# Half of layer 0 over listed columns, one gather for adj and adj^T, norm roots on VectorE

## Chip, cores and metric

One core of a Trainium2 chip. The metric is the device time of one execution in microseconds (us), the median of several. The experiments ran in four calls, each on one chip (numbers 7, 12, 14 and 1, in this order), with seven runs of the kernel before beside them; ratios are to those of the same call. In the profile, PE is TensorE, PEld its weight loads, DVE VectorE, ACT ScalarE, POOL GpSimd, SP SyncE.

## The reference, cut to what matters

```python
# x: 4096 x 256, adj: 4096 x 4096, sparse, with a full diagonal
x = layernorm(x + adj @ (x * W0))                            # layer 0
R = (adj + I) / (adj + I).sum(-1)                            # layer 1, two steps n = 0, 1
for n in range(2):
    A  = top_p(softmax(q(Xa) @ k(Xa).T))                     # keeps a share of 0.9
    Xf = R @ Xf;  Xa = A @ Xa
    Z += Xf @ U1[n].T + Xa @ U2[n].T
x = layernorm(x + layernorm(x + Z) * g + b)
x = layernorm(x + masked_softmax(adj * (x @ Hv)) @ x)        # layer 2
x = layernorm(x + concat(x, adj @ x, edge) @ weight + bias)  # layer 3
#   edge[i] = sum_j adj[i, j] * adj[j, i]
```

adj is so sparse that, for a tile of 128 rows, all nonzero columns fit in 4 to 16 groups of 128 gathered rows. The kernel finds these columns itself ("lists") and multiplies only over them where it can.

## The kernel before

There are 32 row tiles. `CAPS` has the listed column groups of a tile: 16, 10, 8, 7, 7, 6, 7, 5, 6, 5 ... for the first, then 5, and 4 for the last eight. Layer 0 is dense (32 matmuls a tile) and notes on the way which columns are nonzero; attention step 0 then gathers the listed columns of adj^T (`pc`) and of adj (`pr`, needed for `edge`), saves `pc` to DRAM for later layers, and gathers the rows of the features (`xg`).

```python
def pack(I, ps):                       # attention step 0 only
    for m, (a, b) in enumerate(pieces(I)):            # pieces of up to 5 groups
        pc = pools["gat"].tile([P, PIECE, P], F32, name="pc", bufs=4)
        pr = pools["gat"].tile([P, PIECE, P], F32, name="pr", bufs=2)
        for k in range(a, b):
            gather(pc[:, k - a, :], adjT_r, idx_a, col(I, k))      # POOL
            gather(pr[:, k - a, :], adj_r, idx_a, col(I, k))       # POOL
        nc.sync.dma_start(packed[I][m], pc[:, :b - a, :])
        nc.vector.tensor_mul(pr[...], pr[...], pc[...])
        ...  # PE sums pr into edge
def listed_matmul(ps, src, width, I, parts, use=None):
    ...      # per group: gather xg (POOL, six buffers), then one PE matmul
def new_xf(I, psr, old):
    t = ...; nc.vector.tensor_add(t, psr[:, :D], old)
    nc.gpsimd.tensor_scalar_mul(xf, t, rinv[:, I:I + 1])           # POOL
def layernorm(o, y):
    ...      # statistics on VectorE
    nc.gpsimd.tensor_scalar_add(ve, mv[:, 1:2], EPS)               # POOL
    nc.gpsimd.tensor_tensor(rs, ve, neg_half, OP.pow)              # POOL
    nc.vector.tensor_scalar(o, y, mv[:, 0:1], rs, ...)
...
for I in range(NT):                    # step 0
    ...
    weighted_sum(psa, cur[0], X)                                    # PE, dense
    if I >= LAG[0]:
        out_f0(I - LAG[0], r_sum(0, I - LAG[0]))   # pack, listed_matmul, new_xf; PE transposes xf
```

The order of instructions on each engine is fixed when the kernel is built, by a scheduler that may bring an instruction forward past others of its engine.

## Time and profile before

Timed median 4069.91 us (4069.02 to 4073.49). The first profile was of a run of 4129.56 us; a later one spans 4069.7. Stages are read from the timeline: from the start of the ScalarE instruction that writes the first `xa` tile of a step, to the last, and to the last `y` of layer 3.

| stage | first profile | later profile |
|---|---|---|
| layer 0, lists, to the first xa of step 0 | 668.1 | 659.1 |
| step 0, first to last xa | 1183.4 | 1162.4 |
| passage to the first xa of step 1 | 167.2 | 165.3 |
| step 1 | 1510.8 | 1507.7 |
| layers 2 and 3 | 585.9 | 562.7 |

### The profile page before, as it was taken

Reading aid. Unit: us, or ns where it says so; the run is one execution under the profiler, and the core shown is the slowest. Engines: PE = TensorE matmul, PEld = TensorE weight load, DVE = VectorE, ACT = ScalarE, POOL = GpSimd, SP = SyncE. Lnnn points to the kernel's source line nnn. Section 1 sums busy time; section 2 is a strip of 40 time slices with the busy share of each in tenths; the row PEclk is TensorE's granted clock in tenths of the full one; section 3 lists DMA queues with packets and bytes.
Section 4 is the critical chain, followed back from the end, with each engine's and each line's share of the span. In section 5 each row is a group of like instructions: output and inputs, shape, how many; then the busy total and the mean of one; then the engine's idle time right before and its main releaser. Section 6 shows DMA issues by size and latency. Waiting matters only on the chain. (4 is left out here: it accounts for less than half of the span.)

```text
span 4127.7 us, 43235 instructions
## 1 busy us (share of the span) xinstructions
PE 3344.7 (81%) x12988; PEld 2304.1 (56%) x12988; DVE 2409.0 (58%) x7672; ACT 1250.7 (30%) x2837; POOL 1476.9 (36%) x1814
## 2 busy tenths in 40 slices
PE   7999978988889999996887788778888775555576
PEld 5777755656656666663555555445555544433354
DVE  4347446434345455533788888888888889133022
ACT  0000012322223233323444544444444442222011
POOL 1000032255455555524432222211111111577786
PEclk9999987978889999995788878877777877766688
DMA  6444431122222222212211111110000000355454
GB/s 176 141 141 141 141 104 29 45 64 59 63 74 65 66 65 70 66 36 75 74 51 38 39 34 36 35 31 30 29 29 27 27 21 13 114 171 164 129 162 122
DMA packets 291123, 309.34 MB, mean 75 GB/s; under 512 B 34624, under 2 KB 244048, under 8 KB 290880
## 3 DMA queue, kind: packets, MB, share of 16 engines
q1 hardware_dynamic: 234688, 177.31, 14.1%
q0 software_dynamic: 46976, 120.79, 10.4%
q10 hardware_dynamic: 9216, 8.39, 0.7%
q8 instruction: 105, 1.72, 0.2%
q14 instruction: 138, 1.13, 0.1%
HBM read 263.07 MB, written 43.29 MB: 74 GB/s over the span
## 5 line engine op out<-in xcount | busy, mean ns | idle before, releaser
L408 PE MATMUL lg<-kT,qi 64*128 64x512 f32 x1024 | 693.4, 809 | 36.2 <-ACT e L474 14.1
L191 ACT COPY eT<-pt 128x512 f32<-128x512 f32 x512 | 281.6, 588 | 1147.8 <-PE pt L189 1075.0
L213 POOL TENSOR_SCALAR ve<-mv 128x1 f32<-128x1 f32 x160 | 40.0, 250 | 1487.3 <-DVE mv L211 1473.0
L194 PE MATMUL acc<-xa,eT 128*128 128x256 f32 x2048 | 526.1, 414 | 26.3 <-ACT eT L191 26.1
L194 PE MATMUL acc<-x,eT 128*128 128x256 f32 x2048 | 508.9, 395 | 0.0
L178 PE MATMUL acc<-xw,panel 128*128 128x257 f32 x2048 | 483.1, 388 | 23.9 <-DVE xw L113 14.8
L194 PEld LDWEIGHTS acc<-xa,eT 128*128 128x128 f32 x2048 | 413.9, 208 | 129.4 <-ACT eT L191 56.6
L320 POOL DMA_INDIRECT xg<-xd,idx_x x360 | 366.3, 1018 | 281.5 <-PE acc L365 205.5
L189 PE MATMUL pt<-ident,e 128*128 128x128 f32 x2048 | 309.2, 298 | 162.4 <-DVE e L610 143.7
L194 PEld LDWEIGHTS acc<-x,eT 128*128 128x128 f32 x2048 | 378.4, 193 | 105.3 <-ACT eT L191 26.7
L365 PE MATMUL acc<-xg,pc 128*128 128x256 f32 x1080 | 362.3, 462 | 85.0 <-DVE y L668 55.1
L178 PEld LDWEIGHTS acc<-xw,panel 128*128 128x128 f32 x2048 | 379.7, 192 | 89.8 <-issue 26.4
L408 PEld LDWEIGHTS lg<-kT,qi 64*128 64x128 f32 x1024 | 206.1, 235 | 386.8 <-ACT junk L477 161.3
L474 ACT ACTIVATE e<-lg 128x512 f32<-128x512 f32 x512 | 305.6, 599 | 344.6 <-PE lg L408 250.8
L189 PEld LDWEIGHTS pt<-ident,e 128*128 128x128 f32 x2048 | 269.5, 155 | 230.4 <-DVE e L610 195.0
L547 DVE MAX8 cand<-e 128x8 f32<-128x128 f32 x1024 | 226.5, 280 | 287.0 <-ACT e L474 211.3
L320 POOL DMA_INDIRECT pr<-in_adj,idx_a x180 | 259.7, 1443 | 349.6 <-PE acc L339 307.1
L365 PEld LDWEIGHTS acc<-xg,pc 128*128 128x128 f32 x1080 | 230.0, 234 | 152.2 <-DVE y L668 66.7
L172 DVE TENSOR_REDUCE seen<-panel 128x4 bf16<-128x512 f32 x256 | 176.4, 690 | 236.1 <-DMA panel<-in_adjT 235.1
L365 PE MATMUL acc<-xg,pe 128*128 128x257 f32 x360 | 140.8, 566 | 139.8 <-issue 102.0
L204 ACT COPY xT<-ptx 128x256 f32<-128x256 f32 (+1 forms) x160 | 73.0, 456 | 546.8 <-DVE seen L172 283.1
L556 DVE MAX8 cand<-tmp 128x8 f32<-128x128 f32 x1024 | 203.9, 277 | 0.1
(221 smaller groups left out, 4567.9 us busy)
## 6 DMA issues: line engine op xcount, KB each, us to landing
panel<-in_adjT SPq DMA_DIRECT2D x256, 256.0 KB
z<-z SPq DMA_DIRECT2D x128, 128.0 KB
pc<-pk SPq DMA_DIRECT2D x51, 320.0 KB
pc<-pk SPq DMA_DIRECT2D x51, 256.0 KB
xin<-xd SPq DMA_DIRECT2D x96, 128.0 KB
xin<-in_x ACTq DMA_DIRECT2D x64, 128.0 KB
xg<-xd,idx_x POOLq DMA_INDIRECT x360
pk<-pc SPq DMA_DIRECT2D x17, 320.0 KB
```

What stands on the lines that cost most here:

```text
L172: nc.vector.tensor_reduce(seen[:, c * JC:(c + 1) * JC, I], a, AX.X, OP.max, apply_absolute_value=True)
L178: nc.tensor.matmul(ps[:, :width], a[:, k, :], r, start=(j == 0), stop=(j == NT - 1))
L189: nc.tensor.transpose(pt[:, k, :], e[:, j * P:(j + 1) * P], ident)
L191: nc.scalar.copy(eT, pt)
L194: nc.tensor.matmul(ps[:, :D], eT[:, k, :], rhs[j][:, :D], start=(j == 0), stop=(j == NT - 1))
L204: nc.scalar.copy(xT[:, :n, :], pt[:, :n, :])
L320: nc.gpsimd.indirect_dma_start(out=o, out_offset=None, in_=src, in_offset=bass.IndirectOffsetOnAxis(ap=idx[:, c], axis=0))
L365: nc.tensor.matmul(ps[:, :width], pc[:, k, :], xs[k][:, :width], start=(n == 0), stop=(n == CAPS[I] - 1))
L408: nc.tensor.matmul(ps, qi[r, :], kT[r, c * LC:(c + 1) * LC], start=True, stop=True)
L474: nc.scalar.activation(e[:, c * LC:(c + 1) * LC], ps, AF.Exp, accum_out=s8[:, c:c + 1])
L547: nc.vector.max(cand[:, g, :], e[:, g * SEG:(g + 1) * SEG])
L556: nc.vector.max(cand[:, c * (NS // 2) + g, :], w[:, g * SEG:(g + 1) * SEG])
```

## The change

Three parts. (1) Tiles 16 to 31 of layer 0 use lists too; their columns must then be known early, so 64 extra loads of 512 KB look for them during the first five dense tiles. (2) adj and adj^T are interleaved in DRAM (by the host, before the timed execution), so one gather of 1 KB rows brings both; tiles 16 to 31 are gathered in layer 0 and only reloaded in step 0. (3) the roots of the norms of layers 0, 2 and 3 become eight small VectorE operations, and one add of layer 3 moves to VectorE. In step 1 the norms stay on POOL.

```diff
 def pack(I, ps):
-            pc = pools["gat"].tile([P, PIECE, P], F32, name="pc", bufs=4)
+            pc = pools["gat"].tile([P, PIECE, 2, P], F32, name="pc2", bufs=4)
-                gather(pc[:, k - a, :], adjT_r, idx_a, col(I, k))
-                gather(pr[:, k - a, :], adj_r, idx_a, col(I, k))
+                gather(pc[:, k - a].rearrange("p s i -> p (s i)"), pair_r, idx_a, col(I, k))
-            nc.vector.tensor_mul(pr[:, :b - a, :], pr[:, :b - a, :], pc[:, :b - a, :])
+            nc.vector.tensor_mul(pr[:, :b - a, :], pc[:, :b - a, 0], pc[:, :b - a, 1])
@@ layernorm
+        if own:
+            nc.vector.tensor_scalar(ve, mv[:, 1:2], EPS, 0.5, op0=OP.add, op1=OP.mult)
+            nc.vector.tensor_scalar(rs.bitcast(I32), ve.bitcast(I32), -0.5, ..., op0=OP.mult, op1=OP.add)
+            for _ in range(3):
+                t = one("vt")
+                nc.vector.tensor_scalar(t, rs, rs, ve, op0=OP.mult, op1=OP.mult)
+                nc.vector.scalar_tensor_tensor(rs, t, 1.5, rs, op0=OP.subtract, op1=OP.mult)
@@ layer 0
+    def find_columns(J):
+        for b in range(LE, NT, HB):
+            t = pools["loads"].tile([P, HB, P], F32, name="half", bufs=3)
+            nc.scalar.dma_start(t, adjT_v[:, J, b:b + HB, 1])
+            nc.vector.tensor_reduce(seen[:, J, b:b + HB], t, ...)
-    for I in range(NT):
+    for I in range(LE):                    # LE = 16
         ...
+        for J in range(I * NEW, min((I + 1) * NEW, NT)):      # NEW = 7
+            find_columns(J)
+        if (I + 1) * NEW >= NT:
+            ...   # list_columns(1) once, then listed_0(late), one or two per dense tile
-        if I >= LE - 1: ...  three steps of list_columns(0) per tile
-    for _ in lists:
+    for _ in list_columns(0):
         pass
@@ r_sum
-        parts = pack(I, psr[:, D:D + 1]) if n == 0 else unpack(I)
+        parts = pack(I, psr[:, D:D + 1]) if n == 0 and I < LE else unpack(I)
@@ out_3
-        nc.gpsimd.tensor_add(t, t, x3)
+        nc.vector.tensor_add(t, t, x3)
```

## The prediction

> **What bounds the kernel now.** I read the page first, then stretches of the span (busy time of each engine, granted clock, DMA share), then the waits, then the timeline around one wait, and the chain of waits last. The page's second part tells that there are stages with different limits: 40 slices of 103 us.
>
> ```profile
> PE   7999978988889999996887788778888775555576
> DVE  4347446434345455533788888888888889133022
> POOL 1000032255455555524432222211111111577786
> PEclk9999987978889999995788878877777877766688
> DMA  6444431122222222212211111110000000355454
> ```
>
> Slices 1 to 6 are layer 0, dense over all 4096 columns (to 594.7 us in the trace). Slices 7 to 18 are attention step 0 (first output tile at 668.1, last at 1851.5), 19 and 20 the passage to step 1 (2018.7), then step 1 until 3529.5 with DVE at 8, then layers 2 and 3 with POOL at 7 to 8. The profile spans 4127.7 us, 1.4% over the timed 4069.91; I give trace microseconds and neglect that.
>
> By stretches (columns: start and end, length, then busy us of PE, PEld, DVE, ACT, POOL, then granted clock, DMA share, GB/s):
>
> ```profile
> 400.00:500.00 100.00, 95.71 (x462) 77.98 (x461) 41.59 (x91) 6.88 (x24) 4.86 (x12) 1.00 0.48 140
> 900.00:905.00 5.00, 0.04 (x1) 0.04 (x1) 0.28 (x2) 0.00 (x0) 3.97 (x5) 0.62 0.43 137
> 910.00:915.00 5.00, 5.00 (x7) 1.78 (x7) 2.25 (x11) 1.38 (x4) 0.00 (x0) 0.50 0.26 92
> 1300.00:1400.00 100.00, 98.98 (x459) 69.59 (x458) 55.40 (x184) 34.00 (x90) 45.24 (x43) 1.00 0.22 63
> 2100.00:2200.00 100.00, 76.37 (x268) 49.79 (x267) 82.22 (x270) 45.73 (x92) 23.34 (x35) 0.80 0.13 39
> 3900.00:4000.00 100.00, 67.51 (x258) 51.80 (x258) 20.66 (x56) 11.47 (x24) 81.20 (x100) 0.80 0.51 156
> ```
>
> Layer 0 is bound by PE, at full clock, with DMA near half. Step 0 at 1300 is bound by PE too, 33.9 us a tile. But at 900 PE stops, and afterwards it is "busy" at half clock. Who stopped it:
>
> ```profile
> 904.96 0.48 PE L202 MATMUL ptx<-ident,xf 128*128 128x128 f32 x1 [6.31 <-POOL xf L669]
> 925.98 0.94 POOL L320 DMA_INDIRECT pr<-in_adj,idx_a  x1 [16.16 <-PE acc L339]
> 929.11 4.48 DVE L587 SCALAR_TENSOR_TENSOR e<-e,f_u 128x4096 f32<-128x4096 f32 x1
> 929.82 4.59 POOL L320 DMA_INDIRECT pr<-in_adj,idx_a  x1 [0.30 <-issue]
> ```
>
> And in the table of waits (us in total, times, longest us):
>
> ```profile
> POOL pr L320 <- PE acc L339: 307.1, 27, 21.7
> ```
>
> PE waits for POOL's xf; POOL, in order, had been waiting for one of the two pr buffers, freed by PE. That wait came 27 times, 307.1 us in all. The result is visible in the distances of the output tiles: 33.9 us where five columns are listed, 46 to 54 us at tiles 5 to 11, 13 and 20, whose listed tile (about five behind) has 6 to 10.
>
> In layers 2 and 3 POOL issues gathers, and in layer 3 it also does small arithmetic between them:
>
> ```profile
> L828 POOL TENSOR_TENSOR y<-y,xin 128x256 f32<-128x256 f32 x32 | 23.4, 732 | 7.4 <-DVE y L827 6.8
> L213 POOL TENSOR_SCALAR ve<-mv 128x1 f32<-128x1 f32 x160 | 40.0, 250 | 1487.3 <-DVE mv L211 1473.0
> L215 POOL TENSOR_TENSOR rs<-ve,neg_half 128x1 f32<-128x1 f32 x160 | 93.7, 586 | 10.7
> ```
>
> The second number after the bar is the ns of one.
>
> **What the Trainium skill says.** "TensorE: Matmul & The Clock Gate", section Part 1 (the HAM clock gate): after an idle window of about 3.4 us the array runs at half clock until a busy one. Agrees in kind: 6.31 us of wait, then 0.50. The return took longer than one window here (0.50 still at 915 to 920, 1.00 at 935). "SBUF — State Buffer", section Who interferes with whom: a DVE instruction with two SBUF inputs contends with GpSimd's reads. The trace agrees: a gather takes 4.59 us beside the 4.48-us L587, else 0.95. "GPSIMD Engine Reference", section 4.1 Engine selection: elementwise work belongs on VectorE. Agrees: L828 takes 732 ns on POOL, an add of the same 128x256 on DVE (y L668) 409. "DMA: Bandwidth & Descriptors", section Issuing engines are not separate DMA queues: transfers issued by ACT and SP interleave on the same 16 engines. So the new loads on ACT's queue are no extra bandwidth; before has no such pair of heavy queues to check it.
>
> **The change part by part.**
>
> *Layer 0 (to first output tile, 668.1).* Removed: 16 dense tiles of 17.4 us (2.1 MB of panels a tile), 278 us of PE. Added: 16 listed tiles, 72 columns. One fp32 weighted matmul with 257 columns costs about 1.2 us (two records of 0.57), so 4.5 of them 5.4 us with the projection's part neglected, 88 us of PE in all. PE's work falls from about 560 to 370. But to know the columns of tiles 16 to 31, 64 loads of 512 KB come in tiles 0 to 4: 33.5 MB. With panels 5 x 2.1 (and prefetch, 11.8), x 4.9, the copy of xw 4.2 and weights 2, this is 56 MB. The rate at full share I estimate as 140/0.48 = 290 GB/s, so at least 193 us, and with imperfect overlap 225, where PE had needed 87. Then the chain of list_columns for the last 16 tiles: rounds of max and replace, 0.68 + 0.67 + gaps = 1.64 us, some 20 rounds and selections, 35 us, hardly beside anything: 260. Thereafter PE has 10 dense tiles (174) and 88 of listed, and waits at the start for POOL: a listed tile is 4 or 5 pair gathers and as many of xw, 1.25 us each back to back, and the first four hold PE about 20: end at about 541, against 594.7. But now list_columns for the first 16 tiles stands behind all of this, where before it was spread over the last tiles: 32 rounds x 1.64 = 52, and selections, 70 us; then 16 logit matmul groups and keep_few (27) and the weighted sum (28). First output tile at 541 + 125 = 666. Gain: 0, plus or minus 40. PE's saving is eaten by DMA and by the list.
>
> *Step 0.* Gathers per column on POOL fall from three to two for tiles 0 to 15, and to one for 16 to 31, which were gathered in layer 0. pr is no longer filled by a gather, so POOL doesn't wait for it. If PE then never stops, 4 tiles as before (125), 15 tiles x 33.9 + 17 columns over five x 0.69 = 520, the last 12 as before (383, of which 6 for the 40.2 of tile 29): 1028 against 1183, i.e. -155. xg keeps six buffers, which tiles of 7 to 10 columns will overrun, so some stops remain: -120 (35).
>
> *Passage to step 1*, 167 us: four tiles' pack, 16 columns, lose 32 gathers (pc and pr gone; loads from SP instead) x 1.25 = 40 us of POOL, which PE follows. -40 (20).
>
> *Step 1.* Bound by DVE (82%), its layer norms are left on POOL: 0 (10).
>
> *Layers 2 and 3.* Off POOL per tile: in layer 3 the add 0.73, ve 0.25, rs 0.59 and gaps, about 1.7; 32 x 1.7 = 54 at most. Gathers remain 180 x 1.25 = 225 us, so the floor is near 3812 + 225 + 10 and layer 3 ended at 4115: 54 fits in. In layer 2, 0.84 x 32 = 27 at most. DVE gains about 8 small operations, each some 0.15 to 0.2: 1.3 us a tile, at 20% busy it has room. PE has clock 0.80 and 67% busy in layer 3, so not all arrives: -70 (25) for both. The 43.72 us at 3807.50 in the chain of waits is POOL filling the first tiles' gathers of layer 3, and stays.
>
> Sum: 0 - 120 - 40 + 0 - 70 = -230. From 4070: 3840 us.
>
> **Rivals.** (1) Layer 0 gains as PE's work does, 150 us or so, because the loads overlap better than I think: ~3690. For it: DMA has half its share free. Against: 33.5 MB in 5 tiles, and all in order behind panels. (2) Layer 0 gets longer: the loads wait in ACT's in-order stream behind transposes that wait for PE, three buffers only, and PE's clock falls to half while it waits. End of the dense part at 580 to 620, total 3900 to 3930. (3) The waits in step 0 come from xg's buffers and the 4.5-us DVE instruction, not from pr: tiles 5 to 11 stay at 47 us, and the total is ~3950. Against: 307.1 us under pr in the waits, 217.9 under xg. (4) PE at half clock takes POOL's place in layers 2 and 3: +40 over my figure. I chose the middle since (1) and (2) pull in opposite directions.
>
> **Range and chances.** Four terms with 40, 35, 20, 25 give 62 if independent; 1.28 x 62 = 80, and some for what I overlooked: 3740 to 3930. Slower than 3988 (within 2%) needs two rivals together: faster 0.93, same 0.05, slower 0.02.
>
> **What would show it right or wrong.** Layer 0: DMA share above 0.85 and PE under half busy in the first 220 us, first output tile of step 0 near 666; under 600 rival 1, above 700 rival 2. Step 0: tiles 5 to 11 at 34 to 38 us, clock 1.00, no wait of POOL for pr; 47 would be rival 3. Passage near 127 us. Step 1 unchanged at 48.7 us a tile. Layer 3: POOL without L828, L213, L215, over 90% gathers, 6.3 us a tile instead of 8.0. Wrong altogether if POOL's gathers of 1 KB took longer than the 0.95 us of 512 B, which nothing here has measured (an xg row has 1 KB too and takes the same 0.95, so I don't expect it).

## The result

| | before | after |
|---|---|---|
| median us | 4071.7 (4069.02 to 4074.05, 4 runs) | 3967.85 (3963.28 to 3975.08, 4 runs) |
| ratio | | 0.9747, interval 0.9729 to 0.9765 |

A ratio is the mean time of a kernel's fast runs over that of the kernel before's fast runs in the same rounds, so not quite the ratio of the medians. Faster by 2.5%, but 104 us where 230 were forecast: 3967.85 lies outside 3740 to 3930.

Slices of the changed kernel's span, 99 us each (PE, clock and DMA alone):

```profile
PE   4767959998899999998877787878888776555677
PEclk9878977977789999998788878787777777866799
DMA  9956621122222111113211110011000000056565
```

The first two slices show DMA full and PE busy for 4 and 7 tenths; a new hole of PE comes in the sixth slice; slices 9 to 12, the early tiles of step 0, still have the clock at 7 to 8; in the last five PE has gained. The stages of the two kernels, both profiled on one chip (spans 4069.7 and 3972.0):

| stage | before | after | difference | predicted |
|---|---|---|---|---|
| layer 0 to first xa | 659.1 | 663.2 | +4 | 0 |
| step 0 | 1162.4 | 1150.3 | -12 | -120 |
| passage | 165.3 | 144.0 | -21 | -40 |
| step 1 | 1507.7 | 1502.7 | -5 | 0 |
| layers 2 and 3 | 562.7 | 500.9 | -62 | -70 |

One line fails badly: step 0. It misses 108 of the 134 us between these differences (96) and the forecast (230). In the waits (us in total, times, longest), before and then after, on that chip:

```profile
POOL pr L320 <- PE acc L339: 295.9, 27, 18.6
PE ptx L202 <- POOL xf L669: 112.4, 59, 14.3
```

```profile
POOL xg L336 <- PE acc L383: 729.4, 258, 24.4
PE ptx L207 <- POOL xf L711: 90.2, 58, 6.8
```

POOL's wait for `pr`, 296 us, on which the prediction was built, is gone altogether. POOL waits instead for xg's buffers (729.4; before it was 223.4). But PE's wait for xf, the one that costs, only went from 112.4 to 90.2. The timeline of the changed kernel shows how xf comes to be late (start, us, engine, line, instruction, and in brackets the idle time ahead of it with what ended it):

```profile
840.30 0.42 DVE L710 TENSOR_TENSOR y<-acc,xin 128x256 f32<-128x256 f32 x1 [3.22 <-PE acc L383]
...
840.83 0.95 POOL L336 DMA_INDIRECT xg<-xd,idx_x  x1 [0.30 <-issue]
842.08 0.96 POOL L336 DMA_INDIRECT xg<-xd,idx_x  x1 [0.30 <-issue]
843.35 0.95 POOL L336 DMA_INDIRECT xg<-xd,idx_x  x1 [0.31 <-issue]
844.60 0.95 POOL L336 DMA_INDIRECT xg<-xd,idx_x  x1 [0.30 <-issue]
845.58 0.94 POOL L711 TENSOR_SCALAR xf<-y,rinv 128x256 f32<-128x256 f32 x1
...
846.57 0.69 PE L207 MATMUL ptx<-ident,xf 128*128 128x128 f32 x2 [4.40 <-POOL xf L711]
```

y, from which POOL makes xf, is ready at 840.72. POOL first issues four more gathers, back to back 1.25 us apart, and comes to xf at 845.58; PE has then stood for 4.40 us. No wait is put down to POOL in these lines: it is simply busy with something else first. What it gathers there is told by the order of POOL's instructions as built, around this xf (buffer numbers show the tile: 5203 to 5211 belong to this one, 5467 to 5481 are the first six groups of the next):

```text
xg_5205<-xd, xg_5207<-xd, xg_5209<-xd, xg_5211<-xd
xg_5467<-xd, xg_5469<-xd, xg_5471<-xd, xg_5473<-xd, xg_5479<-xd, xg_5481<-xd
xf_5218<-y,rinv
pc2<-pair x3
```

So the next tile's gathers stand in front of this tile's xf. They can be issued only as PE's matmuls for this tile free the six buffers, hence at the very time at which xf is wanted. With 5 groups a tile this fits in; with 6 to 10 it mostly doesn't. Tile by tile, at tiles 5 to 11 and 13 xf starts 4.9 to 7.2 us after y is done, with four to six gathers in between; at all others it starts 0.2 to 1.6 us after it. In the kernel before (later profile) it is 3.7 to 8.5 us at tiles 5 to 11, 13 and 20, and at most 1.6 elsewhere: just the tiles that are slow. The clock then doubles the damage (stretch, length, busy of PE, PEld, DVE, ACT, POOL, granted clock, DMA share, GB/s):

```profile
840.00:850.00 10.00, 5.60 (x12) 2.17 (x11) 2.16 (x9) 2.44 (x7) 7.97 (x9) 0.66 0.41 125
850.00:860.00 10.00, 10.00 (x19) 4.53 (x19) 4.78 (x23) 3.10 (x10) 3.97 (x5) 0.50 0.44 126
```

After the 4.40 us PE is "busy" for 13 us and more at 0.50.

### The profile page after: what moved, and what is told of

It is laid out like the page before. It is cut to its first block, busy times and chain, and to the rows that moved or that the text cites. A ratio compares the mean times of both kernels' runs of the same rounds, so it can differ in the third digit from the quotient of the medians.

```text
span 3968.6 us, 41856 instructions
## 1 busy us (share of the span) xinstructions
PE 3189.8 (80%) x12108; PEld 2148.7 (54%) x12108; DVE 2520.8 (64%) x8408; ACT 1251.9 (32%) x2837; POOL 1198.3 (30%) x1482
## 5 line engine op out<-in xcount | busy, mean ns | idle before, releaser
L336 POOL DMA_INDIRECT xg<-xd,idx_x x360 | 386.4, 1073 | 654.0 <-PE acc L383 591.4
L383 PE MATMUL acc<-xg,pc 128*128 128x256 f32 (+1 forms) x1224 | 418.2, 463 | 144.1 <-DVE y L710 61.9
L383 PEld LDWEIGHTS acc<-xg,pc 128*128 128x128 f32 x1224 | 249.8, 229 | 245.9 <-DVE y L710 75.4
L183 PE MATMUL acc<-xw,panel 128*128 128x257 f32 x1024 | 284.1, 426 | 90.0 <-DVE xw L117 37.1
L230 POOL TENSOR_SCALAR ve<-mv 128x1 f32<-128x1 f32 x64 | 16.5, 258 | 988.6 <-DVE mv L217 987.9
L183 PEld LDWEIGHTS acc<-xw,panel 128*128 128x128 f32 x1024 | 203.6, 209 | 144.3 <-issue 90.8
L336 POOL DMA_INDIRECT pc<-in_pair,idx_a x180 | 171.6, 954 | 137.0 <-DVE idx_a L313 84.2
L336 POOL DMA_INDIRECT xg<-x2d,idx_x x180 | 179.8, 999 | 57.3 <-issue 36.3
L336 POOL DMA_INDIRECT xg<-x3d,idx_x x180 | 171.5, 953 | 72.8 <-issue 23.8
```

Source lines behind the costliest of these rows:

```text
L183: nc.tensor.matmul(ps[:, :width], a[:, k, :], r, start=(j == 0), stop=(j == NT - 1))
L336: nc.gpsimd.indirect_dma_start(out=o, out_offset=None, in_=src, in_offset=bass.IndirectOffsetOnAxis(ap=idx[:, c], axis=0))
L383: nc.tensor.matmul(ps[:, :width], pc[:, k, :], xs[k][:, :width], start=(n == 0), stop=(n == CAPS[I] - 1))
```

## The experiments

### xf on VectorE, fewer buffers, and a call that was slower

First call, four kernels. A second profile of the kernel before:

> The kernel before, unchanged, for a second profile: the first profiled run took 4129.56 us while the timed runs took 4069 to 4074. If that profile was an outlier, this one spans about 4070 us, and the stage that is some 55 us shorter is where the outlier lay; the other stages agree within 5 us. If profiling always lengthens this kernel, it spans 4125 again, and the stage table of the two kernels can't be subtracted as it stands.

xf of step 0 on VectorE in the changed kernel:

```diff
-    def new_xf(I, psr, old):
+    def new_xf(I, psr, old, eng=nc.gpsimd):
-        nc.gpsimd.tensor_scalar_mul(xf, t, rinv[:, I:I + 1])
+        eng.tensor_scalar_mul(xf, t, rinv[:, I:I + 1])
-        return new_xf(I, psr, old)
+        return new_xf(I, psr, old, nc.gpsimd if n else nc.vector)
```

> The changed kernel with the scaling that makes xf moved from POOL to VectorE in attention step 0 only. Theory A (in POOL's order the gathers of the next tile's xg stand ahead of xf; PE waits 4 to 6 us for xf, then works at half clock): tiles 5 to 11 fall from 47 to 53 us to 34 to 38, step 0 from 1152 to about 1040 us, total about 3860 us. Theory B (PE lacks gathered rows, because only six xg buffers are in flight): step 0 stays within 15 us, total 3955 to 3970. Theory C (the weak clock comes from the mix of work itself, without any wait): the same as B.

Fewer xg buffers (the memory has no room for more):

```diff
-  xg = pools["gat"].tile([P, src.shape[1]], F32, name="xg", padded_shape=[P, D + 2])
+  xg = pools["gat"].tile([P, src.shape[1]], F32, name="xg", padded_shape=[P, D + 2], bufs=4 if step_one[0] else 6)
```

> The changed kernel with 4 instead of 6 xg buffers in layer 0 and step 0. Theory A: at most four gathers of the next tile can stand ahead of xf, so the wait is shorter or the same, step 0 between -60 and +20 us. Theory B: more tiles overrun the buffers, the five-column tiles too: step 0 longer by 50 us or more, total above 4010 us. Layer 0's listed tiles may lose some 10 to 30 us under both.

And the same move of xf (the same edit) in the kernel before:

> The kernel before with only the scaling that makes xf moved from POOL to VectorE in attention step 0. Theory A: tiles 5 to 11 fall from 46 to 52 us to about 35 to 40, and the total by 80 to 140 us, to 3930 to 3990, without anything of the change. The theory of the prediction (POOL's wait for the two pr buffers is what costs): PE doesn't wait for xf itself any longer, but the pr wait goes on to hold up POOL's later gathers and thereby PE: less than 40 us gained.

| run | median us | ratio | layer 0 | step 0 | layers 2, 3 |
|---|---|---|---|---|---|
| before_again | 4103.94 | | 664.1 | 1168.0 | 581.2 |
| xf_dve | 4036.28 | 0.9836 | 722.7 | 1079.4 | 574.9 |
| xg4 | 4136.78 | 1.0084 | 704.5 | 1155.0 | 616.8 |
| before_xf_dve | 4075.08 | 0.9928 | 664.7 | 1134.8 | 582.0 |

The kernel before took 4103.53 here (median of 7), on chip 7; in the result and in the other calls it took 4070 to 4074. The totals can't be set against 3967.85, and layers 2 and 3 are 75 us longer in xf_dve than in the changed kernel's first profile, though the edit doesn't reach them. Taken as they stand, xf_dve's total lies under before's by 67 us and fits neither theory's range, and before_xf_dve's 28 us fits the prediction's theory (less than 40) better than theory A. Step 0 alone can be read with care: in xf_dve it is some 70 us shorter than in the changed kernel elsewhere, in before_xf_dve 33 shorter than in before_again, and the number of xg buffers did nothing to it (1155 against 1150 to 1152 of the changed kernel elsewhere, the same distances tile by tile). So theory B, that too few rows are in flight, has nothing for it. With four buffers the built order puts gathers of xg and of pc2 ahead of xf instead; one of PE's waits for xf, at 890.87 in that trace, was 6.31 us. And before_again, profiled, took what the timed runs took: a profile doesn't lengthen the run, and the 4129.56 us of the first one was a slower run of whatever cause.

Second call, with controls:

> The changed kernel once more, as control for the runs of this call. xf_dve ran on a chip where the kernel before took 4103 us and not 4071; there layer 0 was 56 us and layers 2 and 3 75 us longer than in the first profile of the changed kernel, though the edit doesn't reach them. If the chip is the reason, this run shows the same as the other runs of this call in layer 0 and layers 2 and 3, and its ratio to the kernel before differs from 0.9747 if this is again another chip. If the edit was the reason, layer 0 ends at 666 and layers 2 and 3 take 500 here whatever the chip.

> The changed kernel with xf of step 0 on VectorE, now beside the changed kernel on one chip. Theory A (POOL's order puts the next tile's gathers ahead of xf): step 0 about 70 us shorter than in the unedited changed kernel, total 60 to 80 us lower, the other stages equal within 10 us. Theory B (buffers): within 15 us of it.

> The kernel before on the same chip, for a profile that can be subtracted stage by stage from that of the changed kernel: step 0 about 1170 to 1183 us, layers 2 and 3 about 580, if they do not depend on the chip.

| run | median us | ratio | layer 0 | step 0 | passage | step 1 | layers 2, 3 |
|---|---|---|---|---|---|---|---|
| before_2 (one run) | 4071.52 | | 659.1 | 1162.4 | 165.3 | 1507.7 | 562.7 |
| after_again | 3974.24 | 0.9757 | 663.2 | 1150.3 | 144.0 | 1502.7 | 500.9 |
| xf_dve_2 | 3831.6 | 0.9406 | 667.7 | 1017.1 | 131.7 | 1504.9 | 498.7 |

The unedited changed kernel repeats its result, and the stages outside the edit agree within 5 us (the passage is within it: its four tiles have the moved xf too), so the first call's differences there came with that call and not with the edit. On this chip one instruction a tile on another engine is worth 143 us: step 0 is 133 shorter, twice what I expected after the first call. Step 0 in one line for each of before, after, and after with xf moved:

```profile
659.00:1821.00 1162.00, 1098.54 (x4728) 755.05 (x4728) 570.36 (x1893) 355.86 (x932) 544.34 (x502) 0.92 0.21 61
```

```profile
663.00:1813.00 1150.00, 1090.82 (x4616) 742.23 (x4616) 557.66 (x1878) 355.53 (x921) 287.16 (x305) 0.92 0.19 55
```

```profile
668.00:1685.00 1017.00, 1016.94 (x4618) 709.09 (x4616) 565.58 (x1905) 351.55 (x922) 259.35 (x278) 0.99 0.21 62
```

The distances of tiles 5 to 11 are 50, 51, 51, 47, 47, 49, 47 us before, 53, 50, 51, 47, 47, 49, 47 after, and 38, 38, 37, 35, 35, 36, 34 with xf moved. PE's idle time: 1162 - 1099 = 63, 1150 - 1091 = 59, and 0. And its busy time for nearly the same work, 1091 against 1017, at a granted clock of 0.92 against 0.99. Of the 133 us, 59 were waits and 74 were matmuls slowed after waits. The record of granted clock, which knows only 0.5 and 1.0 here, agrees: in step 0 PE was busy at half clock for 171 us in after_again and for 14 in xf_dve_2. Nor did the edit gain by another order of instructions: in step 0, PE and ScalarE ran the same sequence in both, and VectorE's and POOL's differ by the moved xf alone. And the wait itself, in xf_dve_2:

```profile
POOL xg L336 <- PE acc L383: 716.2, 251, 32.7
PE ptx L207 <- POOL xf L711: 29.3, 31, 2.6
```

What is left of it, 29.3, lies in step 1; the difference to 90.2 is 61, about the 59 of above. POOL's wait for xg buffers stays at 716 us and costs nothing now: a large number, over the whole kernel, that says nothing of the end. The move itself is cheap:

```profile
L711 POOL TENSOR_SCALAR xf<-y,rinv 128x256 f32<-128x256 f32 x32 | 30.3, 947 | 14.4 <-DVE mv L217 14.3
L711 DVE TENSOR_SCALAR xf<-y,rinv 128x256 f32<-128x256 f32 x32 | 12.2, 381 | 1.1
```

(the POOL line is step 1's xf, the VectorE line step 0's: 947 and 381 ns.)

### Is it the change that lets the move of xf pay?

> The kernel before with only xf of step 0 on VectorE, a second time, since its first run fell on a chip that was slower. Theory A as first stated: 80 to 140 us below before. After the first run (28 us) I expect rather 30 to 70 us: with 30 gathers for a tile of ten columns (38 us of POOL) and pr's two buffers, POOL remains late in this kernel, and only with the pair gathers does the move of xf free the step.

Measured 3941.98, ratio 0.9682 (0.9665 to 0.970): 128 us below before, inside the first range (80 to 140), above my second guess of 30 to 70. Step 0 took 1038.4. This one move in the old kernel brings more than the whole change did. And its waits:

```profile
POOL pr L320 <- PE acc L339: 202.1, 25, 18.5
PE ptx L202 <- POOL xf L669: 28.5, 29, 3.5
```

PE's wait for xf drops from 112.4 to 28.5 while POOL still waits 202.1 us for `pr`. So the prediction's cause was not one: the `pr` wait can stay, and step 0 is fast. Here too the order of the other instructions in step 0 is that of the kernel before.

### The norm roots

```diff
-    def layernorm(o, y, own=True):
+    def layernorm(o, y, own=False):
@@ out_3
-        nc.vector.tensor_add(t, t, x3)
+        nc.gpsimd.tensor_add(t, t, x3)
```

> The changed kernel with the norms' roots (add and pow) and the add of the last layer put back on POOL. My account puts 70 us of the gain of layers 2 and 3 on these: total 60 to 80 us above the unedited changed kernel, layer 3 back near 8.0 us a tile. Rival: the pair reads or other parts of the change shortened those layers and POOL's arithmetic is hidden: total within 25 us of it.

Measured 4089.39, ratio 1.0033: 115 us above the changed kernel, more than the 60 to 80 expected. Layers 2 and 3 take 563.0 against 500.9, so their whole gain is this part; a tile of layer 3 takes 8.2 us. Layer 3, changed kernel (first profile) and this one:

```profile
3900.00:3950.00 50.00, 43.16 (x189) 31.85 (x188) 36.59 (x129) 8.98 (x19) 37.81 (x41) 0.97 0.61 187
```

```profile
3900.00:4000.00 100.00, 68.29 (x271) 52.60 (x272) 23.92 (x65) 11.49 (x24) 82.45 (x101) 0.88 0.52 161
```

PE works 86% of the time instead of 68 in these stretches; over all of layer 3 it is 81% (165.5 of 204 us) and 69% (165.2 of 241). The rest was a surprise: layer 0 took 717.1, 54 us more. In the listed half of layer 0 POOL has 144 gathers to issue, and a root put among them holds up the tile (VectorE waited 95.8 us for `rs` in that layer 0, and 30.5 in the dense layer 0 of before_2). So the "0" of layer 0 already held this gain.

### Layer 0: listed or dense, and where PE's time went

Layer 0 dense again, both lists bare behind it:

```diff
-    for I in range(LE): ...  # dense tiles, find_columns, listed_0, list_columns(1) and (0)
+    for I in range(NT):
+        ...dense...; out_0(I, ps, xin, X[I])
+        if I >= LE - 1: ...  # three steps of list_columns(0) per tile
+    for _ in list_columns(1): pass
@@ pack: one pc2 and one pr buffer after step 0
@@ r_sum
-        ... if n == 0 and I < LE else unpack(I)
+        ... if n == 0 else unpack(I)
```

> The changed kernel with layer 0 dense over all 32 tiles again (pair gathers for all tiles in step 0, both lists after layer 0, one pc2 and one pr buffer for the last four tiles in the passage); norms and last add stay on VectorE. My account: listing half of layer 0 gained nothing in layer 0 itself, some 12 us in step 0 and 20 in the passage; the second list, now bare, costs 20 to 35: total 20 to 70 us above the changed kernel, 3990 to 4045 (ratio to before 0.98 to 0.993). Rival: the listed half costs time in layer 0: total below 3965.

The extra loads spread thinner in the program, alone and with xf moved:

```diff
-NEW = 7
+NEW = 3
```

> The changed kernel with its extra column loads spread over 11 dense tiles (NEW 3) instead of 5. If layer 0's first 213 us are bound by DMA while PE is half idle, the same bytes lie beside 11 tiles of PE work: the list of the last 16 tiles comes at about 230 us instead of 215, but with only 5 dense tiles left (87 us of PE) instead of 11, and the rest is bound by POOL's 144 gathers, 180 us or more: first output tile 60 to 130 us earlier than 663, total 3845 to 3915. Rival: POOL's gathers at the end cost what the spread gains: total within 25 us of 3970.

> Both edits, loads spread over 11 tiles and xf of step 0 on VectorE. They touch different stages, so the gains should add: total 3700 to 3775 if new3 alone gives 60 to 130 us, otherwise about 3830.

| run | median us | ratio | layer 0 | step 0 | passage |
|---|---|---|---|---|---|
| dense0 | 3966.58 | 0.9742 | 698.7 | 1098.0 | 148.6 |
| new3 | 3961.14 | 0.9732 | 657.1 | 1148.4 | 137.4 |
| new3_xf | 3821.54 | 0.9384 | 658.4 | 1015.4 | 134.0 |

dense0 equals the changed kernel: the listed half of layer 0 gains nothing in the whole as it stands. That missed my range (3990 to 4045): layer 0 was 35 us longer with its bare second list, as expected, but step 0 was 52 us shorter, since its first three slow tiles (30 to 32 us instead of 50 to 53) were fast in the order that this build got. That order is luck, so the run doesn't tell what the listed half is worth in step 0. The rival's condition, under 3965, was not met either.

new3 missed by 46 us or more; its rival (within 25 us) held, and new3_xf came near its second figure (3830). Its first 200 us:

```profile
0.00:100.00 100.00, 44.32 (x98) 25.19 (x98) 48.29 (x92) 0.00 (x0) 12.19 (x76) 0.62 0.96 266
100.00:200.00 100.00, 78.11 (x318) 61.77 (x318) 70.73 (x124) 5.87 (x17) 0.00 (x0) 0.88 1.09 283
```

DMA is just as full (266 and 283 GB/s) and PE just as idle: the scheduler brings the loads forward, so that the last is issued at 216 us, against 208 in after_again, wherever they stand in the program. Only the list, which stands behind the last of them, came later (its end at 306.6 instead of 247.9).

Where PE's saving went can be added up. Layer 0 before, then after, same chip:

```profile
0.00:213.00 213.00, 182.92 (x821) 144.00 (x822) 88.67 (x195) 12.75 (x41) 20.36 (x96) 1.00 0.56 158
213.00:595.00 382.00, 351.12 (x1682) 283.44 (x1681) 200.22 (x453) 27.03 (x93) 41.34 (x85) 0.98 0.48 138
595.00:659.00 64.00, 46.50 (x217) 31.06 (x217) 48.92 (x161) 15.18 (x42) 31.78 (x27) 0.76 0.12 32
```

```profile
0.00:213.00 213.00, 127.06 (x432) 90.44 (x433) 126.83 (x223) 6.25 (x18) 12.16 (x76) 0.91 1.06 276
213.00:300.00 87.00, 54.91 (x240) 40.06 (x238) 47.80 (x147) 5.34 (x20) 40.15 (x58) 0.72 0.47 131
300.00:558.00 258.00, 222.88 (x1110) 173.50 (x1109) 120.80 (x421) 29.03 (x107) 99.38 (x104) 0.92 0.57 160
558.00:600.00 42.00, 2.46 (x11) 2.33 (x11) 39.04 (x84) 0.00 (x0) 0.00 (x0) 0.50 0.00 1
600.00:663.00 63.00, 58.47 (x187) 37.30 (x187) 40.64 (x144) 16.63 (x45) 25.36 (x26) 0.65 0.25 68
```

PE's busy time fell from 580.5 to 465.8, by 115, less than the 190 that I had counted, since more of it now runs at half clock: 124 us of its busy time on the record of granted clock, against 18.5 before. Counted at full clock the work fell by some 170 (an estimate: the record starts at 84 and 26 us). Its idle time rose from 79 to 197: 86 in the loads, 32 and 35 among the listed tiles, 40 at the bare list, 5 after. That is +119, and the saving is gone. Two runs test the two largest pieces. One leaves out half of the extra loads:

```diff
     def find_columns(J):
+        if J >= LE:
+            nc.vector.memset(seen[:, J, LE:], 0.0)
+            return
```

> The changed kernel without the second half of the extra column loads (32 of 64 left out, their column flags set to zero: the result is wrong on purpose, the instructions that follow are the same). If DMA's bytes set the first 213 us, 16.8 MB less at 290 GB/s bring the list of the last 16 tiles, and the first output tile, 40 to 60 us earlier: total 3910 to 3935. Rival: DVE's reductions or ACT's in-order stream set it, and something else fills the gap: less than 20 us.

The first xa came at 628.9, 34 us before 663.2: less than the 40 to 60 of theory, more than the rival's 20. The list of the last 16 tiles was ready at 177.9, 70 us before 247.9, so half of that was lost again in the tiles behind it. The edit also takes out the 32 reductions of these loads on VectorE and their issue on ScalarE, so it doesn't separate the theory from its rival. For the bytes speak the DMA share, 1.06 over the first 213 us and 0.84 in this run, and VectorE's busy time of 127 of these 213 us; ScalarE's in-order stream was not tested by itself. The total (23696.84) means nothing: with incomplete lists the kernel's own check failed and its dense fallback ran behind, which also made the result correct.

The other puts listed tiles beside the list, with xf moved:

```diff
-                n = -(-(NT - late) // (LE - I))
-                for late in range(late, late + n):
-                    listed_0(late)
-                late += 1
-    for _ in list_columns(0):
+                listed_0(late)
+                late += 1
+    lists = list_columns(0)
+    for late in range(late, NT):
+        listed_0(late)
+        for _ in range(7):            # 4 in tail3_xf, which also has NEW = 3
+            next(lists, None)
+    for _ in lists:
         pass
```

> The changed kernel with xf of step 0 on VectorE, and in layer 0 one listed tile after each dense tile from the sixth on, the last six listed tiles after the last dense one, with the list of the first 16 tiles spread between them. If the bare list (about 40 us of idle PE and 28 us of logits at half clock) is what eats the gain of layer 0, the first output tile comes 15 to 50 us before 667: total 3780 to 3815, against 3832 without. Rival: VectorE is full in that stretch, so the list only gets longer: total within 10 us of 3832.

> The same, with the extra loads spread over 11 dense tiles, and 11 of the listed tiles after the last dense one, beside the list of the first 16. Layer 0 then has its two serial parts (loads; the list) beside PE's or POOL's work: first output tile 560 to 620, total 3730 to 3790. Rival: POOL's 144 gathers, 180 us after about 290 us, with their latencies become the bound: first output tile 640 to 660, total about 3820.

And the old kernel with everything that needs neither lists in layer 0 nor pairs:

> The kernel before with xf of step 0, the norms' roots of layers 0, 2 and 3 and the last add on VectorE: all of the gain that needs neither the listed half of layer 0 nor the pair gathers. If these two bring nothing by themselves, 128 and 62 us come off: 3880, within 15. If the pair gathers or the listed half are worth something once POOL no longer holds up xf, this stays 30 to 60 us above 3832, as 3880 does; below 3840 they would cost time.

| run | median us | ratio | layer 0 | step 0 | passage | layers 2, 3 |
|---|---|---|---|---|---|---|
| tail7_xf | 3797.7 | 0.9328 | 630.3 | 1017.1 | 131.5 | 499.7 |
| tail3_xf | 3782.28 | 0.9288 | 622.8 | 1012.7 | 130.6 | 501.3 |
| before_xf_newton | 3887.8 | 0.9545 | 658.3 | 1042.8 | 166.3 | 497.9 |

tail7_xf: 37 us off layer 0, as expected from hiding the list (five listed tiles follow the last dense one by the code, not six). tail3_xf has its total in the range of its theory; its first output tile stands between its theory (560 to 620) and its rival (640 to 660), nearer to theory; it is the fastest version, 7.1% under before and correct. before_xf_newton came out at 3887.8, 8 from its figure: the old kernel with three small moves off POOL. Against it, xf_dve_2 is 1.4% lower by the ratios (0.9406 and 0.9545, of two calls): the pair gathers and listed half together are worth some 55 us once POOL no longer holds up xf, 35 of them in the passage and 26 in step 0, less 9 in layer 0. No run tells the two apart.

## Why the prediction was wrong

- **Layer 0: 0, measured +4.** Right by the mechanism stated: DMA share 1.06 in the first 213 us, half_loads gained 34, the bare list left 40 us of PE idle at clock 0.50. That the sum came out so near (666 foretold, 666.5 and 663.2 measured) is partly luck: the dense and listed part ended at about 557 instead of 541, and what stands behind it took about 106 us instead of 125. The check "DMA share above 0.85" held; "PE under half busy" held only for the first 100 us (46.68), not after (73.57). It left out that the roots on VectorE are worth 54 us here (pool_norm).
- **Step 0: -120, measured -12. This is the step that failed**: "pr is no longer filled by a gather, so POOL doesn't wait for it. If PE then never stops". POOL's wait for pr did vanish; PE's stops didn't. The step took the longest wait in POOL's table for the cause of the wait of PE for xf. Its own lines spoke against it: the pr wait that it shows ended at 925.98, when PE had been running again for 21 us. Before the stop, POOL's last wait for pr had ended at 875.06; from 892.99 on it issued nine gathers back to back, and came to xf, whose y was done at 897.20, only then (the last of them and xf stand below this list). The runs showed in its place that POOL's fixed order has the next tile's gathers ahead of xf: with xf on another engine the idle time of PE goes from 59 us to 0 in the changed kernel, and in the old kernel 128 us are won with the pr wait still there. The gathers of 1 KB took 0.95 us, as assumed. The size was right too: step 0 without stops was put at 1028 us, and xf_dve_2 took 1017.1. The sentence "xg keeps six buffers, which tiles of 7 to 10 columns will overrun, so some stops remain" also named the wrong thing: the stops went with those buffers unchanged.
- **Rival 3** foretold the total ("~3950") and the 47 us of tiles 5 to 11 (46 to 53 were measured), but for a reason, the supply of rows through xg's buffers, that xg4 and xf_dve_2 speak against. It was put aside because 307.1 us stand under pr in the waits against 217.9 under xg. Neither sum measures what the end waited for.
- **Passage: -40, measured -21.** The right sign, half the size; with xf moved it is 34, so 12 of the missing 19 were xf again; the rest stays open. **Step 1: 0, measured -5.** Right. **Layers 2 and 3: -70, measured -62.** Right, and pool_norm gives the whole to the part named; a tile of layer 3 took 6.6 us (204.1 from first to last of 32 tiles, first profile), against 6.3 foretold, and POOL was busy for 73% of that time.
- **"The profile spans 4127.7 us, 1.4% over the timed 4069.91"** was set aside. Some of it is a difference between runs, so before's first profile could not be subtracted from after's: their spans differ by 159 us.

The two instructions of POOL ahead of PE's stop, from the trace that the prediction read:

```profile
902.98 0.94 POOL L320 DMA_INDIRECT xg<-xd,idx_x  x1 [0.30 <-issue]
903.95 0.95 POOL L669 TENSOR_SCALAR xf<-y,rinv 128x256 f32<-128x256 f32 x1
```

What stays open: in the first call the same move of xf gained 28 us in the old kernel instead of 128, and xf_dve took 4036 instead of 3832, while the kernel before was slower by only 0.8%. In xf_dve's trace ScalarE took its logits 3.5 us apart where PE's records have them one microsecond apart, and about one in eight of PE's semaphore events was missing (2282 of 2584 are there). The same loss is in all four traces of that call and in the first profile of the kernel before, the 4129.56-us run (2417 of 2772), and in none of the other 13 traces. So long times and incomplete records go together, and whether the chip or a state of the recording made them is not shown. I have no cause for it. The prediction was read from one of these incomplete traces; its stages were up to 23 us longer than in the later profile, its waits much the same (307.1 us under pr, 295.9 later).

## What to carry to other kernels

Ask of a long wait who stands behind it: a wait of an engine that is ahead of the others costs nothing, however long (here POOL's 716 us in xf_dve_2), and a short wait of the engine that bounds the stage can cost twice itself through the clock (here 59 us of waits went with 74 us of slower matmuls). Before taking away what an in-order engine waits for, read its built order between the input of the critical small operation and that operation; if gathers of the next tile stand there, move the operation to another engine. When work is moved to be earlier, check what becomes bare behind it, and compare profiles of one call only.

## What the Trainium skill lacked or had wrong

- "TensorE: Matmul & The Clock Gate", Part 1, has a busy window of about 3.4 us bring the clock back. After the wait of 4.40 us it was still 0.50 throughout the stretch 850 to 860, with PE busy since 846.57; the record of granted clock has this stretch at half clock last 20.5 us. In the sum of step 0, 59 us of waits went with 74 us of slower matmuls.
- "GPSIMD Engine Reference", section 4.1, puts two-input work on GpSimd at about twice VectorE's time and one-input work roughly at line rate. The first holds (732 ns against 409 for the add that the prediction compares); the scaling of xf, one input with a factor per row, took 947 ns against 381, so 2.5 times. And the reason that counted is not in that section: on POOL the operation stands behind gathers of 1.25 us each, and moving it was worth 128 to 143 us where its own time differs by 32 x 0.57 = 18.
- "DMA: Bandwidth & Descriptors", Specifications, has about 358 GB/s as HBM's limit per core. With runs of 512 bytes from two queues the trace shows 271 and 289 GB/s at a DMA share above 1; I found a measured rate for that pattern on this chip in no page. My 290, worked out from a share of 0.48, was good.
- No page that I found says that one kernel's times can differ so between chips or calls: the same old kernel took 4104 us in one call and 4070 to 4074 in three others and in the result, and a variant 4036 in the one and 3832 in another. Nor does one say that traces of such slow runs can lack one in eight of the semaphore events.
